# A four-layer network on one core: layer 1's bands from one row at the end of the preparation, a bias table shared with GpSimd, and layer 1's first image in the input weights' place

## The chip, the core and the metric

The kernel runs as one launch on one core of a Trainium2 chip. A core has five engines that run their own instruction lists side by side: TensorE (PE, matrix products into PSUM), VectorE (DVE), ScalarE (ACT), GpSimd (POOL) and SyncE (SP, which here only issues DMAs). Each takes its list strictly in order, so an instruction that waits for a semaphore holds all that stands behind it on its engine. DMAs are issued from SP, ACT and POOL. The metric is the device time of the launch in microseconds (us).

## The reference

The input `x` is 4 x 8 x 512 x 512 in float32. Four layers follow each other, and each adds its result to its own input after a group normalisation (`_gn`, four groups of two channels).

```python
def lif(x):
    def step(v, xt):
        v = v + (xt - v) / TAU
        spk = (v >= V_TH)
        v = v * (1.0 - spk)
        return (v, spk)
    _, s = jax.lax.scan(step, jnp.zeros_like(x[0]), x)
    return s
...
q, k, v = (heads(lif(bn(x @ W.T))) for each of q, k, v)
scores = jnp.einsum('tbhnd,tbhmd->tbhnm', q, k) * scale
bias = bias_table[rel].transpose(2, 0, 1)
scores = scores + bias[None, None]
out = jnp.einsum('tbhnm,tbhmd->tbhnd', scores, v)
out = lif(out)
out = out * gate_scale + gate_shift
out = lif(bn(out @ Wp.T))
...
x = x + layer0(_gn(x))        # the attention above
x = x + conv13x13(_gn(x), w)  # layer 1, one kernel per channel, reflected border
x = x + conv3x3_quantised(_gn(x))
x = x + conv3x3(_gn(x))
```

The first block is shortened: `lif` also has a surrogate for gradients that doesn't change its value, and the line for q, k, v stands for three.

## The kernel before

**Layer 0** works through 32 steps `(b, t)`, b over 8 channels and t over 4 time steps. In a step, four tiles of 128 x 512 of x are transposed on PE and normalised on DVE into `xn` (`transpose`), and multiplied with the input weights `w_v`, `w_k` and `w_q` in this order, four column blocks each (`project_in`, L464: PE multiplies, DVE takes `potential` and the spikes, GpSimd adds a constant to the state). `attend` forms k'v (`ps_kv`), multiplies it with q (`ps_a`, L492), and adds the position bias times v (`ps_b`, L500), for which the bias table is held three times in bfloat16, `toep` 0 to 2: the rounded value, the rounded rest, and the rest of that. `project_out` (L527) multiplies with the output weights `wp` and writes the sum to DRAM as layer 1's input `x1d`, with reflected borders. The loop runs with n from -1: it attends to step n and projects step n + 1. The loads of x (SP, ten buffers) go into the order of the loop.

Ahead of it stands the **preparation**. `load(0)` brings the first x; `bands1` builds layer 1's bands; the three weights are loaded from ACT's queue; `statistics` counts group 0 (`bn_stats`, L393) and `norm_of` makes mean and `grstd` from it: sum, matmul `gps_x` (L178), subtraction, squares, sum, matmul, power on GpSimd (L195). `prepare_in` scales a weight with its batch norm (`diag` L310, `ps_free` L311, multiplication L323, ACT's doubling L324). `prepare_bias` fills `toep` (loads L335, casts on ACT L339, L341 and L343, subtractions on DVE L340 and L342), two heads in flight, since `hankel` and `rest` have two slots each. `prepare_out` scales the output weights and splits them in two (L375 to L381). Where the code says `issue_after`, the order of issue is held behind the named instruction; else a scheduler orders instructions by its own estimate of when they are ready, and the order on each engine is fixed when the kernel is built.

**bands1** makes the matrices by which layer 1's 13 x 13 convolution becomes matrix products: for each of 16 output rows of a window, four products of a constant that slides the taps (`c13`) with the taps of all channels (L673), 64 products in all, copied out of PSUM by ACT and DVE (L682) into a tile in `h_q`'s place, and written to DRAM as `band1d` (L686), since the place is needed again.

**Layer 1** (`Layer1`) is made after layer 0's tiles are given up. It loads `band1d` and an identity `eye` (L706, L709, SP), loads the taps again, sums them (`w_rows`, `ps_sum` L719, `w_sum` L721) and runs 32 images `(b, t)`. For each image SP loads two halves of 917 KB (L732), DVE makes `bt`, the band of channel b times the image's normalisation `r1`, plus the identity (L740), PE multiplies (L750, 64 records), ACT adds `off` on the way out (L757), DVE takes statistics (L759 to L761), and ACT and POOL write to `x2d` (L766). Three image buffers and four PSUM banks rotate. `norm1(3)`, which normalises the last group of layer 0's output, and `weights23`, which prepares layers 2 and 3, stand in the code behind image group 0, but the scheduler is free to put their instructions ahead of it.

**Layers 2 and 3** run interleaved after layer 1 and write the output.

Of the kernel before, what the change touches and what calls it, by code (L numbers as in the profile page):

```python
# [42 lines left out]
P = 128  # L43
T, B, N, D, H = 4, 8, 512, 512, 8
DH = D // H
NC = N // P
# [80 lines left out]
def network(ctx: ExitStack, tc: tile.TileContext, i: dict, out: bass.AP):  # L127
# [81 lines left out]
    band1d = tc.dram_tile([K1_P, B * SHIFTS * M1], F32, name="band1d")  # L209
# [9 lines left out]

    with ExitStack() as s:  # L220
        layer0(s, tc, i, x_in, x1d, ident, block, avg, group_stats, st1, norm1, band1d)
# [15 lines left out]
    with ExitStack() as s:  # L237
        ps_1 = s.enter_context(pool("ps_2", space=PSUM))
        layer1 = Layer1(s, tc, i, x1d, x2d, avg, group_stats, r1, mr1, st2, m2, r2, most, band1d, ps_1, pool)
        layer1.group(0)  # L240
        for g in range(1, G):
            if g == 1:
                norm1(G - 1, ps_1)
                w23 = weights23(tc, i, late, early["y"], ps_1, ident)
            layer1.group(g)
        layer1.next_norm(G - 1)
    with ExitStack() as s:
        layers23(
            s, tc, x2d, out, ident, ind, mask2, avg_same, group_steps, m2, r2, most, w23, early, pool
        )  # L250


def layer0(s, tc, i, x_in, x1d, ident, block, avg, group_stats, st1, norm1, band1d):
# [9 lines left out]
    wT = {n: wpool.tile([P, NC, D], F32, name=f"w_{n}") for n in "vkq"}  # L263
# [16 lines left out]
    def load_weights(n):  # L280
        nc.scalar.dma_start(wT[n], i[f"wT_{n}"].rearrange("(c p) e -> p c e", p=P))
# [44 lines left out]
    def prepare_bias():  # L326
# [6 lines left out]
        for h in range(H):  # L333
# [8 lines left out]
            nc.vector.tensor_sub(r, r, dst[1])  # L342
# [244 lines left out]

    load(0)
    bands1(tc, i, band1d, ps_mm, work, state)
    load_weights("v")  # L590
# [3 lines left out]
    load_weights("k")  # L594
    load_weights("q")
    for k in range(NC):
        transpose(0, k)
    prepare_in("v")
    first = [prepare_in("k")]
    h_of = {n: state.tile([P, NC, N], F32, tag=f"h_{n}", name=f"h_{n}") for n in "vkq"}  # L600
    for n in range(-1, last + 1):
        b, t = steps[max(n, 0)]
        if n >= 0:
            with tc.issue_after(did) if n == 0 else ExitStack():
                so = attend(spikes, t)
            residual = load_x(b, t, "xr")
        if n + 1 <= last:
# [9 lines left out]
            if g + 1 < G:  # L617
                t_next, pair = divmod(j, PAIR)
                statistics(
                    g + 1, t_next, pair, load_x((g + 1) * PAIR + pair, t_next, "xs")  # L620
                )
        for a, name in enumerate("vkq"):
            for c in range(NC):
                if n + 1 <= last:
                    did = project_in(name, c, xns[n + 1], spikes, steps[n + 1][1])
                if (n, name, c) == (-1, "v", 0):
                    first += [did, potentials[0]]
# [14 lines left out]
        if n < 0:  # L642
            with ExitStack() as behind:
# [3 lines left out]
                prepare_out(load_out())  # L647
            for name in "op":
                h_of[name] = state.tile([P, NC, N], F32, tag=f"h_{name}", name=f"h_{name}")


def bands1(tc, i, band1d, psum, work, state):

    nc = tc.nc
    n_w, n_c = K1 + 2 * (PH - 1), i["c13"].shape[1]
    both = work.tile([K1, n_c + B * n_w], F32, tag="q", name="c13")
    c13 = both[:, :n_c]
    nc.scalar.dma_start(c13, i["c13"])
    w1 = both[:, n_c:].rearrange("k (c d) -> k c d", c=B)
    nc.vector.memset(w1, 0.0)  # L660
    taps = w1[:, :, PH - 1 : PH - 1 + K1]
    nc.scalar.dma_start(taps, i["w1"].rearrange("k (c d) -> k c d", c=B))

    band = state.tile([K1_P, B, SHIFTS, M1], F32, tag="h_q", name="band1")
    n_r = 4
    n_s = SHIFTS * PH
    c13 = c13.rearrange("k (f j) -> k f j", f=PH)
    for r0 in range(0, W1_OUT, n_r):
        ps = psum.tile([K1_P, n_r, B, n_s], F32, tag="mm", name="ps_band")
        for r in range(r0, r0 + n_r):  # L670
            at = (W1_OUT - 1 - r) * PH
            for f in range(PH):
                nc.tensor.matmul(  # L673
                    ps[:, r - r0, :, :].rearrange("p c z -> p (c z)"),
                    lhsT=c13[:, f, at : at + K1_P],
                    rhs=w1[:, :, f : f + n_s],
                    start=f == 0,
                    stop=f == PH - 1,
                )
        for z in range(SHIFTS):  # L680
            copy = nc.vector.tensor_copy if z % 2 else nc.scalar.copy
            copy(  # L682
                band[:, :, z, r0 * PH : (r0 + n_r) * PH].rearrange("p c (r o) -> p c r o", o=PH),
                ps[:, :, :, z * PH : (z + 1) * PH].rearrange("p r c o -> p c r o")[:, :, :, ::-1],
            )
    nc.scalar.dma_start(band1d, band.rearrange("p c s m -> p (c s m)"))  # L686


class Layer1:
    def __init__(  # L690
        self, s, tc, i, x1d, x2d, avg, group_stats, r1, mr1, st2, m2, r2, most, band1d, ps_1, pool
# [4 lines left out]
            r2=r2, most=most, ps_1=ps_1,  # L696
        )
        self.ps_c = s.enter_context(pool("ps_c", 4, space=PSUM))
        wpool = s.enter_context(pool("w1"))
# [5 lines left out]
        self.band = wpool.tile([K1_P, B, SHIFTS, M1], F32, name="band1")  # L705
        nc.sync.dma_start(self.band.rearrange("p c s m -> p (c s m)"), band1d)  # L706
        self.eye = wpool.tile([K1_P, SHIFTS, M1], F32, name="eye")
        n_eye = SHIFTS * M1
        nc.sync.dma_start(  # L709
            self.eye.rearrange("p s m -> p (s m)"), i["c128"][:K1_P, i["c128"].shape[1] - n_eye :]  # L710
        )
        taps = wpool.tile([K1, B, K1], F32, name="taps")
# [489 lines left out]
```

## Time and profile before

| | |
|---|---|
| median of 3 runs | 3027.5 us (3026.57 to 3029.91) |
| profiled execution | 3032.56 us, span 3030.8 us, mean PE clock 0.984 |
| PE busy | 2915.8 us (96%) |
| DVE busy | 2212.7 us (73%) |
| ACT busy | 553.9 us (18%) |
| POOL busy | 1039.8 us (34%) |
| first projection (L464) | at 52.2 us |
| layer 0 ends, layer 1's products begin | 2117.1 us, 2131.9 us |
| layer 1's products end | about 2583.9 us |

A busy time is the time in which an engine had an instruction in work. Matmul ends are modelled, so a busy PE is not one at its peak, and an average over the span hides that each stage has a limit of its own. A product in float32 shows as two records. Times of single instructions come from one profiled execution, and its span is compared with itself; the runs give the time.

### The profile page before, as it was taken

What the parts mean: (1) busy time and instruction counts of PE and PEld (TensorE: products, weight loads), DVE (VectorE), ACT (ScalarE), POOL (GpSimd) and SP (SyncE); (2) the same over time, 40 slices, a digit from 0 to 9 for tenths busy, and PEclk for the clock granted to TensorE, in tenths of its full rate; (3) what the DMA queues carried; (4) which work ended last, traced back from release to release, by engine and by line L of the source; (5) the groups of instructions that cost most, each with busy time, mean ns of one, the idle gap of its engine ahead of it and who ended that gap; (6) DMA issues with size and microseconds to landing.
All of it is one profiled execution on the core that took longest, in us unless ns stands there. A gap on an engine that the chain in (4) does not pass through costs nothing. (4 is left out here: it accounts for less than half of the span.)

```text
span 3030.8 us, 38824 instructions
## 1 busy us (share of the span) xinstructions
PE 2915.8 (96%) x13993; PEld 1450.6 (48%) x13993; DVE 2212.7 (73%) x3793; ACT 553.9 (18%) x867; POOL 1039.8 (34%) x1963
## 2 busy tenths in 40 slices
PE   8999999999999999999999999999899999688989
PEld 6555555555555555555555555555333333234433
DVE  5997688788769868867976886786555556886760
ACT  1400010000000001000000000100111111766664
POOL 1242233333224323323422433332211112676651
PEclk9999999999999999999999999999899999889999
DMA  5222222221212222222221111111877878698986
GB/s 185 74 85 64 71 71 64 64 67 61 84 57 71 64 64 71 70 64 64 68 61 55 46 54 50 50 50 44 207 216 199 215 210 239 144 189 216 227 195 172
DMA packets 275702, 327.37 MB, mean 108 GB/s; under 512 B 23600, under 2 KB 171192, under 8 KB 275285
## 3 DMA queue, kind: packets, MB, share of 16 engines
q1 hardware_dynamic: 211930, 235.77, 29.0%
q0 software_dynamic: 23776, 62.35, 7.5%
q10 hardware_dynamic: 39803, 26.77, 3.0%
q8 instruction: 110, 1.80, 0.3%
q14 instruction: 83, 0.68, 0.1%
HBM read 210.60 MB, written 103.17 MB: 104 GB/s over the span
## 5 line engine op out<-in xcount | busy, mean ns | idle before, releaser
L464 PE MATMUL ps_in<-w_v,xn 128*128 128x512 f32 x1024 | 460.7, 599 | 2.5 <-issue 2.2
L464 PE MATMUL ps_in<-w_k,xn 128*128 128x512 f32 x1024 | 450.2, 592 | 1.0 <-DVE v_k L429 0.7
L464 PE MATMUL ps_in<-xn,w_q 128*128 128x512 f32 x1024 | 449.6, 592 | 0.1
L750 PE MATMUL ps_conv<-x,bt 112*64 112x512 f32 x2048 | 445.4, 594 | 0.0
L500 PE MATMUL ps_b<-toep,vtok 128*64 128x512 bf16 x3072 | 371.8, 382 | 0.0
L412 ACT ACTIVATE h_q<-v_q,c_half 128x512 f32<-128x512 f32 x96 | 69.3, 722 | 1543.6 <-DVE v_q L408 1222.3
L549 POOL COPY x1s<-x1s 128x2 f32<-128x2 f32 (+1 forms) x1024 | 226.5, 275 | 295.6 <-DVE x1s L538 295.6
L437 POOL TENSOR_TENSOR h_v<-h_v,c_v 128x512 f32<-128x512 f32 x96 | 123.0, 1281 | 575.3 <-DVE h_v L436 540.8
L527 PE MATMUL ps_out<-wp,so 128*128 128x512 f32 x1024 | 308.8, 444 | 0.0
L1104 PE MATMUL ps_conv<-x,band_t 64*64 64x512 f32 x2040 | 271.7, 609 | 30.2 <-POOL x L1097 14.3
L464 PEld LDWEIGHTS ps_in<-w_k,xn 128*128 128x128 f32 x1024 | 194.1, 190 | 222.4 <-issue 204.7
L464 PEld LDWEIGHTS ps_in<-xn,w_q 128*128 128x128 f32 x1024 | 191.8, 190 | 220.1 <-issue 212.9
L464 PEld LDWEIGHTS ps_in<-w_v,xn 128*128 128x128 f32 x1024 | 190.0, 190 | 216.4 <-issue 211.0
L750 PEld LDWEIGHTS ps_conv<-x,bt 112*64 112x64 f32 x2048 | 150.1, 135 | 286.7 <-issue 286.4
L500 PEld LDWEIGHTS <-vtok 128*64 128x64 bf16 x3072 | 209.5, 110 | 124.0 <-issue 3.6
L527 PEld LDWEIGHTS ps_out<-wp,so 128*128 128x128 f32 x1024 | 192.5, 188 | 94.0 <-issue 58.3
L967 POOL COPY u<-x 128x512 f32<-128x512 f32 (+1 forms) x172 | 200.2, 1197 | 108.0 <-DMA x<-x 71.8
L538 DVE SCALAR_TENSOR_TENSOR x1s<-v_p,xr 128x256 f32<-128x256 f32 x256 | 186.5, 769 | 14.4 <-DMA x<-x1s 3.1
L766 POOL DMA_DIRECT2D x<-xo x128 | 71.4, 564 | 341.1 <-ACT xo L757 326.6
L1104 PEld LDWEIGHTS ps_conv<-x,band_t 64*64 64x64 f32 x2040 | 105.1, 135 | 145.5 <-issue 93.7
L195 POOL TENSOR_TENSOR grstd_x<-grstd_x,neg_half 128x1 f32<-128x1 f32 (+1 forms) x28 | 21.9, 784 | 437.7 <-DVE grstd_x L194 435.6
L757 ACT ACTIVATE xo<-ps_conv,off 128x512 f32<-128x512 f32 x128 | 88.0, 688 | 445.8 <-PE ps_conv L750 387.0
(182 smaller groups left out, 3664.2 us busy)
## 6 DMA issues: line engine op xcount, KB each, us to landing
x<-x SPq DMA_DIRECT2D x64, 917.0 KB
x<-x SPq DMA_DIRECT2D x168, 256.0 KB
x<-x1s POOLq DMA_DIRECT2D x128, 262.0 KB, 2.6
x<-in_x SPq DMA_DIRECT2D x128, 256.0 KB
xr<-in_x SPq DMA_DIRECT2D x128, 256.0 KB
out<-o SPq DMA_DIRECT2D x164, 192.0 KB
xs<-in_x SPq DMA_DIRECT2D x112, 256.0 KB
x<-xo ACTq DMA_DIRECT2D x128, 128.0 KB
```

What stands on the lines that cost most here:

```text
L412: nc.scalar.activation(h, v, AF.Identity, bias=c_col, scale=0.5)
L437: nc.gpsimd.tensor_add(h, h, c_twice[n])
L464: mm = nc.tensor.matmul(ps, lhsT=lhsT, rhs=rhs, start=k == 0, stop=k == NC - 1)
L500: nc.tensor.matmul(pb[two * DH : (two + 1) * DH, :], lhsT=v[:, c, h * DH : (h + 1) * DH], rhs=toep[z][:, h, u : u + N], start=c == 0 and z ...
L527: nc.tensor.matmul(ps, lhsT=so[:, k, c * P : (c + 1) * P], rhs=wpT[z][:, k, :], start=k == 0 and z == 0, stop=k == NC - 1 and z == 1,)
L538: nc.vector.scalar_tensor_tensor(own, v.rearrange("p (g v) -> p g v", g=PH)[:, two, :], 1.0, by_phase[:, two, :], op0=ALU.is_ge, op1=ALU.add,)
L549: nc.gpsimd.tensor_copy(x1[:, f, u : u + n], x1[:, fm, um - n + 1 : um + 1][:, ::-1])
L750: nc.tensor.matmul(ps[q * M1 : (q + 1) * M1, :], lhsT=bt[:, z, :], rhs=xt[:, w0 : w0 + N_PS1, z : z + NV], start=z == 0, stop=z == SHIFTS - 1,
L757: nc.scalar.activation(xo[:, a, :], ps, AF.Identity, bias=off[:, t : t + 1])
L766: engine.dma_start(bass.AP(dst.tensor, dst.offset + (q * n_half * W1_OUT * B + b) * D + f * NV, [[B * D, W1_OUT], [W1_OUT * B * D, n_half] ...
L967: nc.gpsimd.tensor_copy(u[:n_p, j, :].rearrange("p (v g) -> p v g", g=PH), x[:, j, :].rearrange("p (g v) -> p v g", g=PH),)
L1104: mm = nc.tensor.matmul(ps[j][b * HALF : (b + 1) * HALF, :], lhsT=band[half, b, dx, :], rhs=x3[half, s0 + j, dx : dx + D], start=dx == 0, ...
```

## The change

Layer 1's bands are no longer built row by row. `bands1` makes one row by four products into 52 partitions, fills `band1d` with zeros by a DMA from a small zero tile, and writes the row 16 times on top of it, each time four partitions and 128 elements further on, by one DMA whose source is repeated. It also sums the taps (`w_sum`) there, and loads `eye`. It stands as the last part of the preparation, and its scratch is in `h_p`'s place. The element order of the band changes, so `bt` is made by four DVE instructions of 112 x 64 instead of one of 112 x 256.

The second subtraction of the bias table goes from DVE to GpSimd. `w_v` is loaded from SP behind the first x; `w_k` and `w_q` are loaded once `w_v` is prepared, and `k` is prepared behind v's first projection. The statistics of the next group for n = -1 go behind the preparation of the output weights.

The input weights move to a pool that outlives layer 0. In the last step, `w_v`'s place takes the band, and the place of `w_k` and `w_q` takes layer 1's first image; its `bt` is made there too. `norm1(3)` and `weights23` are held behind the first image's last product and last statistic.

```diff
-    band1d = tc.dram_tile([K1_P, B * SHIFTS * M1], F32, name="band1d")
+    band1d = tc.dram_tile([K1_P, W1_OUT * B * SHIFTS * PH], F32, name="band1d")
...
             if g == 1:
-                norm1(G - 1, ps_1)
-                w23 = weights23(tc, i, late, early["y"], ps_1, ident)
+                with ExitStack() as behind:
+                    for op in layer1.started:
+                        behind.enter_context(tc.issue_after(op))
+                    norm1(G - 1, ps_1)
+                    w23 = weights23(tc, i, late, early["y"], ps_1, ident)
...
-    wT = {n: wpool.tile([P, NC, D], F32, name=f"w_{n}") for n in "vkq"}
+    n_x1 = W1_N * X1_U
+    wv = shared.tile([P, NC * D], F32, tag="v", name="w_v")
+    wkq = shared.tile([P, max(2 * NC * D, n_x1)], F32, tag="kq", name="w_kq")
...
-            nc.vector.tensor_sub(r, r, dst[1])
+            nc.gpsimd.tensor_sub(r, r, dst[1])
...
+    def start_layer1():
+        band = shared.tile([K1_P, W1_OUT, B, SHIFTS, PH], F32, tag="v", name="band1")
+        nc.sync.dma_start(band.rearrange("p r c s o -> p (r c s o)"), band1d)
+        x = shared.tile([K1_P, W1_N, X1_U], F32, tag="kq", name="x1_0_0")
+        load_image(nc, x, x1d[0][0])
+        bt = shared.tile([K1_P, SHIFTS, M1], F32, name="bt_0_0")
+        image_bands(nc, bt, band, 0, r1[:, 0, 0:1], eye)
+        return band, eye, x, bt
...
     load(0)
-    bands1(tc, i, band1d, ps_mm, work, state)
-    load_weights("v")
+    load_weights("v", nc.sync)
     statistics(0, 0, 0, xs[0])
     statistics(0, 0, 1, load_x(1, 0, "xs"))
     batch_norms()
-    load_weights("k")
-    load_weights("q")
     for k in range(NC):
         transpose(0, k)
-    prepare_in("v")
-    first = [prepare_in("k")]
+    with tc.issue_after(prepare_in("v")):
+        load_weights("k", nc.scalar)
+        load_weights("q", nc.scalar)
+    first = []
...
             residual = load_x(b, t, "xr")
+            if n == last:
+                head = start_layer1()
...
                 if (n, name, c) == (-1, "v", 0):
-                    first += [did, potentials[0]]
+                    first += [prepare_in("k"), did, potentials[0]]
...
                 prepare_out(load_out())
+                next_group(n)
+                bands1(tc, i, band1d, w_sum, eye, ps_mm, state)
...
+    nc.vector.memset(zeros, 0.0)
+    rest = band1d.rearrange("p (r m) -> p r m", r=W1_OUT)
+    nc.scalar.dma_start(rest, zeros.unsqueeze(1).to_broadcast([K1_P, W1_OUT, P]))
+    ps = psum.tile([n_p, P], F32, tag="mm", name="ps_band")
+    for f in range(PH):
+        nc.tensor.matmul(
+            ps, lhsT=c13[:, f, :], rhs=w1[:, :, f : f + n_s], start=f == 0, stop=f == PH - 1
+        )
+    nc.vector.tensor_copy(
+        band.rearrange("p (m o) -> p m o", o=PH), ps.rearrange("p (m o) -> p m o", o=PH)[:, :, ::-1]
+    )
+    row = W1_OUT * P
+    nc.scalar.dma_start(
+        bass.AP(band1d.tensor, band1d.offset, [[row, n_p], [PH * row + P, W1_OUT], [1, P]]),
+        band.unsqueeze(1).to_broadcast([n_p, W1_OUT, P]),
+    )
+    nc.vector.tensor_reduce(rows, w1, AX.X, ALU.add)
+    nc.vector.memset(zeros[:K1, :], 1.0)
+    ps = psum.tile([P, B], F32, tag="mm", name="ps_sum")
+    nc.tensor.matmul(ps, lhsT=zeros[:K1, :], rhs=rows, start=True, stop=True)
+    nc.vector.tensor_copy(w_sum, ps)
...
-        bt = self.bp.tile([K1_P, SHIFTS, M1], F32, tag="bt", name=f"bt_{b}_{t}")
-        nc.vector.scalar_tensor_tensor(
-            bt, self.band[:, b, :, :], self.r1[:K1_P, g, t : t + 1], self.eye,
-            op0=ALU.mult, op1=ALU.add,
-        )
+        if (b, t) == (0, 0):
+            xt, bt = self.head
+        else:
+            xt = self.xp.tile([K1_P, W1_N, X1_U], F32, tag="x", name=f"x1_{b}_{t}")
+            load_image(nc, xt, self.x1d[t][b])
+            bt = self.bp.tile([K1_P, SHIFTS, M1], F32, tag="bt", name=f"bt_{b}_{t}")
+            image_bands(nc, bt, self.band, b, self.r1[:, g, t : t + 1], self.eye)
```

## The prediction

> **What bounds the kernel now.** I read the busy slices first. TensorE (PE) is at 9 tenths in nearly every slice of layers 0 and 1, so what counts there is where it idles or does work that could go. A table by stretches (columns after the length: PE, weight loads, DVE, ACT, POOL busy, each with a count; granted clock; DMA share; GB/s) finds two such places:
>
> ```profile
> 0.00:10.00 10.00, 2.82 (x13) 2.85 (x14) 3.43 (x12) 0.00 (x0) 4.41 (x8) 1.00 0.80 267
> 10.00:20.00 10.00, 10.00 (x49) 10.00 (x48) 5.61 (x14) 1.55 (x2) 0.00 (x0) 1.00 1.05 391
> ...
> 120.00:130.00 10.00, 6.63 (x30) 3.20 (x30) 9.55 (x18) 6.41 (x11) 0.00 (x0) 0.85 0.26 81
> ...
> 2120.00:2130.00 10.00, 1.18 (x4) 1.00 (x4) 8.50 (x23) 0.00 (x0) 7.71 (x23) 0.52 0.81 184
> 2130.00:2140.00 10.00, 8.71 (x26) 3.44 (x28) 2.08 (x11) 0.00 (x0) 1.04 (x1) 0.63 1.04 208
> ```
>
> The timeline of the start says what the "busy" PE does there (start, length, engine, line, operation):
>
> ```profile
> 7.18 13.96 PE L673 MATMUL ps_band<-c 13*112 13x128 f32 x64 [7.18 <-DVE st L393]
> 15.72 0.17 DVE L175 TENSOR_REDUCE gsum_x<-st 128x1 f32<-128x16 f32 x1
> 21.07 0.59 PE L178 MATMUL gps_x<-gsum_x,avg 128*128 128x1 f32 x2
> 23.40 13.99 PE L673 MATMUL ps_band<-c 13*112 13x128 f32 x64
> 38.18 0.55 POOL L195 TENSOR_TENSOR grstd_x<-grstd_x,neg_half 128x1 f32<-128x1 f32 x1 [30.98 <-DVE grstd_x L194]
> 52.23 2.04 PE L464 MATMUL ps_in<-w_v,xn 128*128 128x512 f32 x2 [2.19 <-issue]
> ```
>
> The reader should see 128 records of layer 1's bands ahead of everything. The statistics of the first tile were summed at 15.7 but their two matmuls stood behind 14.0 us of bands each, so the first projection began at 52.2. The chain that ended last shows the second place, the passage from layer 0 to layer 1 (start, length, what):
>
> ```profile
> 2117.11 3.88 DMA x<-x1s
> ...
> 2126.67 0.60 PE ps_sum L719 x2
> ...
> 2131.30 0.59 PE gps_x L178 x2
> 2131.88 45.07 PE ps_conv L750 x192
> ```
>
> Layer 0's last matmul ends at 2117.1; the convolution begins at 2131.9, behind ps_sum and norm1's gps_x, which are in front of it on PE. From 2122 to 2136 the finer table gives a clock of 0.50.
>
> **What the Trainium skill says.** "TensorE: Matmul & The Clock Gate", What's actually happening: an idle array falls to half clock and wins full clock back by sustained work. The trace agrees: 0.50 above, and x192 took 45.07 us where later x64 take 13.88, so 41.6; 3.4 us were lost. "SBUF — State Buffer", Who interferes with whom: a DVE instruction with two SBUF inputs and a GpSimd one that reads SBUF block each other for a whole instruction. The trace fits: the 128x896 subtraction takes 1.08 us, but 1.56 at times, and GpSimd's 128x512 addition 1.27, or 2.0 while those run. "DMA: Bandwidth & Descriptors", Anatomy of one DMA: about 2 us are fixed, most of it confirmation of the write. A bias-table load took 3.8 us from issue (56.4) to the cast that waited for it (60.2), with data. "GPSIMD Engine Reference", Elementwise: a two-input operation costs about twice DVE's. Here 1.27 against 0.7, so it agrees.
>
> **Part by part: the start.** (1) Bands leave the front: 128 records, 27.9 us of PE, 16 copies. Of w_v, w_k and w_q only w_v now loads at once, on SP behind x; so before the statistics are complete 3.4 MB must come (x, w_v, xs at 1.05 each, constants 0.2). At the table's 267 GB/s for 10 us and 391 after, that is 11.8 us, against 15 now. The last bn_stats ends at 12.5. The chain (reduce, matmul, copy, three small DVE steps, reduce, matmul, add, power) is some 4 us by its rows; four w_v multiplications of 0.62 stand between its steps: 18.7. Then xn at 0.80: first projection at about 20, 32 us earlier. (2) Some is given back. k's preparation, formerly ahead of the projections, now stands behind v's first: eight diag of 0.24 and four multiplications (2.5 us) on DVE, while PE's second group waits for their steps; w_k is issued only after v's preparation (19), so it lands near 26. DVE also gets four bn_stats (2.5 us) of xs that it used to do at 16 to 21, when idle. Stepping through both queues gives 22 us for v's phase instead of 16.4: k starts at 42 instead of 68.6, 26 earlier. (3) Bias table: eight L342 subtractions (1.08) leave DVE, 8.6 us, and become GpSimd's, at 896/512 x 1.27 = 2.2 us free, 3.3 if blocked as above. But ACT takes its casts in order, toep_2 of a head ahead of toep_1 of the next, so a pair of heads costs six casts (5.6), two GpSimd subtractions and one of DVE: 11 us. In the trace pairs start at 69.0, 81.4, 90.7, 99.9, about as far apart. So the last cast stays some 23 us earlier: 86.5, not 109.4. (4) The preparation's tail, where the trace shows PE waiting for ACT behind the output weights:
>
> ```profile
> 124.47 0.59 ACT L510 ACTIVATE v_o<-ps_a 128x512 f32<-128x512 f32 x1
> 125.11 0.41 PE L492 MATMUL ps_a<-q,kvb 128*64 128x512 f16 x2 [2.62 <-ACT v_o L510]
> ```
>
> gets the new bands: 10 small matmul records, DVE about 1.1 us (two memsets, reduce, copy, memset, copy), and four loads and writes on ACT. ACT's write of the band waits for the 896 KB of zeros to land, with the wp casts behind it; DVE's memset of ones waits for the same, with the weights' second pass and the next tile's xn behind; ps_sum on PE waits for that memset, with v's next projection behind. The zeros go out in 512 B pieces. Layer 1 moves such pieces at 242 GB/s in its densest stretch: 3.8 us, and 2 fixed, 7 with the input loads beside it. PE waits 4 to 5 us there, but DVE's wp work ends hardly earlier, so 1 to 4 us stick. Upper bound: a 128 KB write from POOL lands in 5.9 us in the issue table; seven of these in a row would be 41. I take 7. So PE's third head pair starts at 106, not 126.5: **20 us** gained, bounds 8 and 28 (32 less the 4 that must stick).
>
> Hidden: statistics moved by half a step in layer 0 (PE is busy 298.9 of 300 us from 1200 to 1500); the eye load, 112 KB on ACT.
>
> **The passage.** The band (SP, waits for w_v's last reader) is read back behind the xr loads. Its bt stands on DVE directly behind an x1s; w_v's last matmul starts near 2063, 896 KB take about 5 us, DVE gets there after 6: 0 to 1 us. The image goes where w_k and w_q were, released at 2096: two loads of 917 KB, 9 us at 200 GB/s, ready by 2107. The convolution then follows ps_out as soon as DVE has read the last two ps_out (1.39 us from 2116.5): 2118.0 instead of 2131.9. That is 13.9 us, exactly one image of PE time, and 3.4 us of clock. SP's next image now waits for tiles read last at 2109 (toep), not for the eye load (25.6 us of SP waiting now); it lands well before 2132. norm1 and weights23 go behind image 0 on DVE, which is busy 54 us of 100 in layer 1; their two gps_x cost PE 0.8 us there. bt becomes four 112x64 instead of one of 0.48 us; at up to 0.3 each that is 0.7 more of a 13.9 us image: hidden. **16.5 us**, bounds 11 and 17.5.
>
> Sum: 20 + 16.5 = 36.5 from the span of 3030.8, so 2994; this execution was 3032.6 by the clock of the runs, 0.17% over their median of 3027.5. Taken off the median: **2991**. Layers 2 and 3 move along unchanged.
>
> **Rivals.** (a) The tail is worse: zeros of 15 to 20 us, or GpSimd's subtractions above 3.3 us, eat 8 to 13 of the start: 2999 to 3005. For: DVE is full from 60 to 100 already (10.00, 9.56, 10.00, 9.88). Against: GpSimd is idle there half the time. (b) The start comes almost whole: 28 to 30, 2981. For: PE's order puts other work into the waits. Against: the in-order casts. (c) The passage fails: image 1 is late, as its second half was issued 8 us after the first in this trace, behind another queue's load: 20 alone, 3007. Against: its queue slots are old ones. (d) Slower: the zeros hold ACT, DVE and PE at once. Only above 7 + 36.5 = 43.5 us does that turn the sign, and 50 us for 0.2% (6 us); even 41 leaves 3025. (e) That the change doesn't do what it says: excluded for the order of PE, where L673's records are gone from the front.
>
> **How the numbers follow.** Forecast 2984 to 2999: 0.66. (a) 0.14, (b) 0.11, (c) 0.03, no change 0.03, (d) 0.03. Range 2981 to 3004 leaves out about a fifth: the far ends of (a) and (b), (c), no change and (d). No change means within 0.2%, about what a measurement of this kernel can tell.
>
> **What would show it.** First ps_in<-w_v near 20; k's near 42; last toep cast near 86; ps_a's wait for ACT near 104; ps_conv within 2 us of the last ps_out and no clock of 0.5 after it. A ps_sum wait above 10 us, DVE idle on a bands write, or a hole after image 0 would make it wrong.

## The result, and the profile after

The changed kernel takes 3004.6 us (median of 4 runs, 3004.4 to 3006.8); the kernel before took 3028.7 in the 4 runs beside it. The ratio is 0.9919, with a 95% interval of 0.9902 to 0.9936. It is faster by 24 us; the forecast was 36.5 us and 2991 (2981 to 3004). The marks in one row of the tables below come from one profiled execution. Two executions of one kernel differ by some 2 us in the start (170.3 and 172.4 below). Over all kernels, whatever their edit, the rest of layer 0 (second step to last ps_out) varies by 6.5 us, and layers 2 and 3 from 439 to 449 us. So the start and the passage are read from the trace, and the whole from the ratios.

Four marks in the trace carry what follows: ACT's first `v_o` of the third pair of heads (end of the preparation), the first `v_o <- ps_a` on DVE of the second time step, the start of layer 0's last `ps_out`, and from there to the start of the last `ps_conv` record of layer 1 (passage and layer 1).

| us | first v_o | second step | last ps_out | to last ps_conv |
|---|---|---|---|---|
| before | 124.5 | 183.2 | 2116.7 | 466.5 |
| after | 111.2 | 170.3 | 2105.5 | 451.5 |
| forecast, by its sum | 104 | 163 | 2096.7 | 450.0 |

The lines behind the first two rows (the first v_o of before stands in the prediction; in the view by tile the figures are count, shortest/median/longest ns, first and last start), first before, then after:

```profile
183.18 0.69 DVE L512 SCALAR_TENSOR_TENSOR v_o<-ps_a,h_o 128x512 f32<-128x512 f32 x1
L527 PE MATMUL ps_out<-wp,so x1024: 388/394/799, 133.9 to 2116.7; 128*128 128x512 f32 x171
...
170.32 0.68 DVE L533 SCALAR_TENSOR_TENSOR v_o<-ps_a,h_o 128x512 f32<-128x512 f32 x1
L548 PE MATMUL ps_out<-wp,so x1024: 388/395/801, 118.9 to 2105.5; 128*128 128x512 f32 x171
L797 PE MATMUL ps_conv<-x,bt x2048: 589/591/644, 2106.0 to 2557.0; 112*64 112x512 f32 x187
```

The passage brought 15.0 of the 16.5 us expected. The start brought 13.3, 12.9 and 11.2 where 20 were expected. The table of stretches of the kernel after (columns as ahead of the prediction) shows both:

```profile
0.00:10.00 10.00, 3.35 (x11) 2.10 (x12) 4.17 (x17) 1.28 (x1) 4.41 (x8) 1.00 0.79 268
10.00:20.00 10.00, 5.27 (x19) 4.01 (x18) 7.50 (x23) 0.03 (x1) 0.55 (x1) 1.00 0.64 226
90.00:100.00 10.00, 6.75 (x45) 4.56 (x45) 8.00 (x23) 2.12 (x3) 0.96 (x1) 0.94 0.63 177
100.00:110.00 10.00, 8.40 (x18) 4.34 (x19) 7.76 (x15) 2.71 (x5) 0.55 (x1) 0.72 0.55 152
...
2110.00:2120.00 10.00, 9.96 (x48) 3.04 (x44) 4.88 (x15) 0.16 (x1) 6.58 (x20) 1.00 0.78 184
```

From 90 to 110 PE, DVE and ACT are all part idle, and the clock falls to 0.72. That fits a wait for something outside them. At the passage nothing is left of the clock of 0.50. PE's timeline says where the start's gain stood at each point:

```profile
21.58 1.91 PE L485 MATMUL ps_in<-w_v,xn 128*128 128x512 f32 x2
...
43.91 1.45 PE L485 MATMUL ps_in<-w_kq,xn 128*128 128x512 f32 x3
...
101.60 0.56 PE L738 MATMUL ps_sum<-bands 13*128 13x8 f32 x2 [3.75 <-DVE gsum_x L175]
...
112.71 0.82 PE L521 MATMUL ps_b<-toep,vtok 128*64 128x512 bf16 x5
...
169.40 0.41 PE L513 MATMUL ps_a<-q,kvb 128*64 128x512 f16 x2 [3.34 <-DVE kvb L506]
...
2106.00 13.95 PE L797 MATMUL ps_conv<-x,bt 112*64 112x512 f32 x64
2120.59 1.94 PE L797 MATMUL ps_conv<-x,bt 112*64 112x512 f32 x8 [0.63 <-ACT xo L804]
```

v starts 30.7 us earlier than before, k 24.7, as forecast within 2 us. The third pair of heads starts at 112.7, 13.8 earlier and not 20; before it was at 126.5:

```profile
126.48 3.97 PE L500 MATMUL ps_b<-toep,vtok 128*64 128x512 bf16 x20
```

So the loss lies between, and a little more follows at 169. ACT's own timeline (ACTq is its issuing of DMAs) shows what it waited for:

```profile
94.48 0.69 ACTq L719 DMA_DIRECT2D band1d<-bands  x1
...
101.05 0.37 ACTq L730 DMA_DIRECT2D band1d<-bands  x1
101.46 1.14 ACT L400 CAST wp<-wp_k 128x512 fp32r<-128x512 f32 x2 [5.66 <-DVE gsum_x L175]
...
111.24 0.59 ACT L531 ACTIVATE v_o<-ps_a 128x512 f32<-128x512 f32 x1
```

L719 writes the zeros to DRAM, L730 the row of bands into them. L730 is issued 6.57 us after L719, as it must wait until the zeros have landed, and ACT's casts of the output weights stand behind it. (The releaser printed, gsum_x, is not it: in the second execution of this kernel the view names the DMA of band1d at this place, with 5.60 us.) ACT's first `v_o` of the third pair stands at the end of that row of casts, at 111.24.

### The profile page after: what moved, and what is told of

It is laid out like the page before. It is cut to its first block, busy times and chain, and to the rows that moved or that the text cites. A ratio compares the mean times of both kernels' runs of the same rounds, so it can differ in the third digit from the quotient of the medians.

```text
span 3002.9 us, 38667 instructions
## 1 busy us (share of the span) xinstructions
PE 2889.0 (96%) x13873; PEld 1426.6 (48%) x13873; DVE 2225.3 (74%) x3875; ACT 551.0 (18%) x859; POOL 1054.3 (35%) x1971
## 5 line engine op out<-in xcount | busy, mean ns | idle before, releaser
L485 PE MATMUL ps_in<-xn,w_kq 128*128 128x512 f32 x1024 | 453.0, 595 | 4.8 <-DVE v_q L441 3.7
L485 PE MATMUL ps_in<-w_kq,xn 128*128 128x512 f32 x1024 | 450.1, 593 | 1.6 <-DVE v_k L450 1.6
L485 PEld LDWEIGHTS ps_in<-w_kq,xn 128*128 128x128 f32 x1024 | 194.3, 190 | 223.1 <-issue 205.3
L485 PEld LDWEIGHTS ps_in<-xn,w_kq 128*128 128x128 f32 x1024 | 192.1, 191 | 227.4 <-issue 211.8
L1153 PE MATMUL ps_conv<-x,band_t 64*64 64x512 f32 x2040 | 276.1, 612 | 24.4 <-ACT o L1162 13.8
L1016 POOL COPY u<-x 128x512 f32<-128x512 f32 (+1 forms) x172 | 198.2, 1185 | 104.5 <-DMA x<-x 56.7
L1153 PEld LDWEIGHTS ps_conv<-x,band_t 64*64 64x64 f32 x2040 | 112.3, 136 | 135.9 <-issue 94.2
L1051 PE MATMUL ps_conv<-xq,band 64*64 64x512 bf16 x1020 | 138.8, 399 | 32.1 <-DVE xq L1031 32.0
```

Source lines behind the costliest of these rows:

```text
L485: mm = nc.tensor.matmul(ps, lhsT=lhsT, rhs=rhs, start=k == 0, stop=k == NC - 1)
L1016: nc.gpsimd.tensor_copy(u[:n_p, j, :].rearrange("p (v g) -> p v g", g=PH), x[:, j, :].rearrange("p (g v) -> p v g", g=PH),)
L1051: mm = nc.tensor.matmul(ps[half, :], lhsT=w["band2"][half, 0, dx, :], rhs=xq[half, j, dx + 1 : dx + 1 + D], start=dx == 0, stop=dx == 2,)
L1153: mm = nc.tensor.matmul(ps[j][b * HALF : (b + 1) * HALF, :], lhsT=band[half, b, dx, :], rhs=x3[half, s0 + j, dx : dx + D], start=dx == 0, ...
```

## The experiments

All edits are to the changed kernel unless another base is named. Theory: the missing 8 to 9 us of the start are lost (T1) to GpSimd's subtractions, (T2) to the zeros and the bands at the end of the preparation, (T3) to the moved statistics. The marks of all runs, and the ratio to the kernel before:

| us | first v_o | second step | last ps_out | to last ps_conv | ratio, 95% interval |
|---|---|---|---|---|---|
| after | 111.2 | 170.3 | 2105.5 | 451.5 | 0.9919, 0.9902 to 0.9936 |
| after, again | 113.2 | 172.4 | 2106.4 | 452.0 | 0.9917, 0.9901 to 0.9932 |
| subtraction on DVE | 106.8 | 168.8 | 2104.4 | 452.1 | 0.9917, 0.9902 to 0.9932 |
| zeros early | 107.0 | 163.9 | 2096.3 | 451.6 | 0.9886, 0.9868 to 0.9904 |
| zeros early, again | 105.9 | 162.8 | 2095.8 | 450.9 | 0.9904, 0.9887 to 0.9920 |
| no bands | 104.9 | 162.9 | 2096.4 | 451.5 | 0.9881, 0.9864 to 0.9897 |
| statistics early | 114.7 | 175.3 | 2112.7 | 451.8 | 0.9940, 0.9924 to 0.9956 |
| zeros early, k early | 110.2 | 167.1 | 2101.7 | 451.4 | 0.9901, 0.9884 to 0.9918 |
| zeros early, DVE | 104.5 | 163.9 | 2099.8 | 452.2 | 0.9885, 0.9869 to 0.9902 |
| zeros early, in pairs | 108.9 | 166.6 | 2100.1 | 451.8 | 0.9884, 0.9860 to 0.9907 |
| ones of their own | 112.1 | 171.7 | 2105.2 | 451.6 | 0.9924, 0.9909 to 0.9938 |
| row from GpSimd | 108.5 | 171.0 | 2102.4 | 451.5 | 0.9915, 0.9900 to 0.9929 |
| kvb first | 110.7 | 167.0 | 2101.5 | 451.4 | 0.9908, 0.9893 to 0.9923 |
| row from GpSimd, kvb first | 105.0 | 164.0 | 2094.9 | 451.3 | 0.9879, 0.9864 to 0.9894 |
| image late | 112.5 | 172.2 | 2108.9 | 460.6 | 0.9947, 0.9929 to 0.9964 |
| whole passage back | 114.0 | 173.0 | 2109.9 | 460.4 | 0.9954, 0.9938 to 0.9969 |

**Subtraction on DVE.**

```diff
-            nc.gpsimd.tensor_sub(r, r, dst[1])
+            nc.vector.tensor_sub(r, r, dst[1])
```

> The changed kernel with the second subtraction of the bias table back on VectorE, all else as it is (3004.6 us there). Theory T1, that the missing 9 us of the start go to GpSimd's eight subtractions (VectorE stretched from 0.42 to about 2 us beside them, and ScalarE's in-order casts waiting 2 to 4 us for each of them): the last bias cast ends 3 to 6 us before 91.9, and the time is 2999 to 3002. Rival, the forecast's own sum (a pair of heads 11 us with GpSimd, more without): the table ends later, 94 to 97, and the time is 3007 to 3010.

The last cast of the table began at 84.0 instead of 91.0: GpSimd makes the table 7 us later. But TensorE's wait at ps_sum grew from 3.75 to 7.5 us, and the ratio is the same, 0.9917. Each theory had half of it: the table was earlier, the time was not. That GpSimd's cost was only hidden behind the zeros was the next guess; the run with both edits, below, doesn't bear it out.

**Zeros early.** `zeros` is the still empty tile of `eye`; the sum of the taps takes the existing `ones`.

```diff
                         statistics(0, 1, 1, load_x(1, 1, "xs"))
+                        zeros = eye.rearrange("p s m -> p (s m)")[:, :P]
+                        nc.vector.memset(zeros, 0.0)
+                        nc.sync.dma_start(band1d..., zeros.unsqueeze(1).to_broadcast(...))
...
-    nc.scalar.dma_start(rest, zeros.unsqueeze(1).to_broadcast([K1_P, W1_OUT, P]))
...
-    nc.vector.memset(zeros[:K1, :], 1.0)
```

> The changed kernel with the zeros of layer 1's bands written to DRAM early, from the still empty tile of eye, on SyncE's queue behind the first potential, and the existing tile of ones in place of the rewritten zeros; the row of bands itself stays at the end of the preparation. Theory T2, that TensorE's wait of 3.75 us at ps_sum (the ones are written only when the fill has landed) and ScalarE's 5.7 us before the casts of the output weights are on the path: that wait is gone and the time is 3000 to 3002. Rival: the path through the end of the preparation is the bias table and VectorE, and the wait lies beside it: 3003.5 to 3005.

ACT's timeline with the zeros early:

```profile
98.97 0.62 ACT L400 CAST wp<-wp_k 128x512 fp32r<-128x512 f32 x1 [1.19 <-DVE wp_k L396]
...
100.25 0.36 ACTq L732 DMA_DIRECT2D band1d<-bands  x1
...
106.95 0.59 ACT L531 ACTIVATE v_o<-ps_a 128x512 f32<-128x512 f32 x1
```

The casts start before the row is written, not behind it. Layer 0 ends at 2096.3, 20.4 us before the kernel before: the forecast's 20. That is more than T2 expected, so the zeros cost more than the one wait. All eight runs of this kernel (2991.0 to 3001.90, both of its rows in the table) lie below all nine of the changed kernel (3001.92 to 3009.5), the nearest two by hardly anything.

**Bands left out.** As zeros early, and the row of bands isn't made: layer 1 works with empty filters (band zero, `w_sum` one), with the same instructions.

```diff
-    ps = psum.tile([n_p, P], F32, tag="mm", name="ps_band")
...
-    nc.vector.tensor_copy(w_sum, ps)
+    nc.vector.memset(w_sum, 1.0)
```

> The changed kernel with the zeros written early and the row of bands left out altogether (band stays zero, w_sum is set to one, so layer 1 is computed with empty filters; the instructions of the layers are the same). This is the most that moving the bands away from the end of the preparation can bring. Theory T2: 4 to 6 us less than the changed kernel, 2998.5 to 3000.5. Rival, that the loss lies before 92 (GpSimd) or after 112: 3003 to 3005.

No gain over the zeros early at the end of layer 0 (2096.4 and 2096.3). The row itself costs next to nothing; its zeros do.

**Statistics early.**

```diff
-            if n >= 0:
-                next_group(n)
+            next_group(n)
...
-                next_group(n)
                 bands1(tc, i, band1d, w_sum, eye, ps_mm, state)
```

> The changed kernel with the second group's first statistics (four loads of xs and their VectorE work) back at their old place, ahead of v's first projection. Theory T3, that moving them behind the preparation pushes the next loads of xs into the first time step, where VectorE waits 1.9 us for them and TensorE 3.3 us at 169 for kvb: that wait is gone, v's projections start up to 1 us later, and the time is 3002 to 3003.5. Rival, that the moved work was in the way of the first projections: those start 3 us later (near 25) and the time is 3006 to 3009.

The rival came nearer. v's first projection wasn't later (20.5), but the marks are 2 to 7 us later and TensorE still waited 3.1 us for kvb. By the marks it was a gain that these statistics moved (the intervals of the ratios overlap), and their move is not what makes kvb late.

**k early**, with the zeros early.

```diff
-    with tc.issue_after(prepare_in("v")):
-        load_weights("k", nc.scalar)
-        load_weights("q", nc.scalar)
-    first = []
+    prepare_in("v")
+    first = [prepare_in("k")]
```

and the two loads straight behind `batch_norms()`.

> The kernel with the zeros written early (2993.7 us in its own runs), with k's weights loaded on ScalarE's queue straight behind the statistics and prepared ahead of v's projections, as in the kernel before. Theory, that k's late preparation (TensorE waits 2.6 us for VectorE's scaled weights of k, and k starts at 46.4 where the forecast said 42) costs the start: k starts 2 to 3 us earlier, and the time is 1 to 3 us less. Rival, that VectorE and ScalarE with the bias table set the pace from 50 on, and the wait for k only moves: v's first projection is later (25 to 28), the table ends at 91 as before, and the time is within 1 us or up to 3 us more.

v starts at 32.2, k at 47.6 (46.4), the second step 3 to 4 us later. The rival, and a little more than it said (2998.0 against 2993.7 and 2997.2; the ratios don't tell them apart): by the marks, loading k behind v was right, and TensorE's 2.6 us for k's weights are the small price.

**Image late.** Image (0, 0) is taken from layer 1's pools like the others; band and eye stay ahead.

```diff
-        x = shared.tile([K1_P, W1_N, X1_U], F32, tag="kq", name="x1_0_0")
-        load_image(nc, x, x1d[0][0])
...
-        if (b, t) == (0, 0):
-            xt, bt = self.head
-        else:
+        if True:
```

> The changed kernel with layer 1's first image and its bands taken from layer 1's own pools again, as all later images are (band and eye stay loaded ahead). Theory, the forecast's passage: the image can be loaded only when layer 0's pools have been given back, so that TensorE stands 8 to 14 us after its last product of layer 0, and restarts with a lower clock; last product of layer 0 at 2105.9 as in the changed kernel, first of layer 1 near 2118; time 12 to 17 us more. Rival, that band and eye were the long part of it: the image's load alone costs 4 to 8 us.

9.1 us more from the last ps_out to the end of layer 1; 8 by the times. PE's timeline shows where:

```profile
2101.58 7.76 PE L548 MATMUL ps_out<-wp,so 128*128 128x512 f32 x32
2110.51 1.93 PE L791 MATMUL ps_conv<-x,bt 112*64 112x512 f32 x4 [1.18 <-DVE bt L755]
2116.66 1.98 PE L791 MATMUL ps_conv<-x,bt 112*64 112x512 f32 x4 [4.22 <-DMA x<-x]
```

Four records find their half of the image, the next wait 4.2 us for the other, and from 2118 to 2122 the clock is 0.50. That is less than the theory's 12 to 17, and at the upper end of the rival's 4 to 8: the image is the larger part, but not all.

**Zeros early, subtraction on DVE**: both edits.

> The kernel with the zeros written early, and the second subtraction of the bias table back on VectorE as well. Theory T1 and T2 together: the table ended 7 us earlier without GpSimd, which was hidden behind the zeros (TensorE's wait at ps_sum grew from 3.7 to 7.5 us); with neither, the last cast ends near 85, TensorE's third pair of heads comes 4 to 7 us earlier than the 108.1 with the zeros early, and layer 0 ends near 2091: 2987 to 2990 us. Rival, that VectorE, which then does eight subtractions of 1.05 us more, is the limit at the end of the preparation too: layer 0 ends within 2 us of 2096, and the time is that of the zeros early, 2991.5 to 2995.

The rival. The ACT cast groups of the view by tile (count, shortest/median/longest ns, first and last start), first of the zeros early, then with the subtraction on DVE too:

```profile
L364 ACT CAST toep<-rest x8: 922/938/939, 55.5 to 91.2; 128x896 bf16<-128x896 f32 x8
```

```profile
L364 ACT CAST toep<-rest x8: 922/938/940, 53.1 to 82.7; 128x896 bf16<-128x896 f32 x8
```

The table ends 8.5 us earlier, the first v_o comes 1.4 to 2.5 us earlier, and the second step begins at the same 163.9. With the eight subtractions DVE is busy for 19.96 of the 20 us from 60 to 80.

**Casts in pairs**, with the zeros early: `prepare_bias` issues both first casts of a pair of heads, then both second, then both third.

```diff
+            for src, r, dst, h in pair:
+                nc.scalar.copy(dst[1], r)
+                nc.gpsimd.tensor_sub(r, r, dst[1])
+            for src, r, dst, h in pair:
+                nc.scalar.copy(dst[2], r)
```

> The kernel with the zeros written early, GpSimd still doing the second subtraction, but the bias table issued for two heads at once: both first casts, both second casts, both third casts, so that ScalarE has a cast of the other head to do while GpSimd subtracts. Theory, that ScalarE's wait in order is what GpSimd costs (17.1 us idle behind the second cast in the kernel with the zeros early): the table ends 4 to 7 us earlier, near 86, and layer 0 ends 3 to 6 us earlier. Rival, that VectorE's stretched instructions beside GpSimd are the cost: the table ends within 2 us of 92.1 and the time is within 1.5 us of the zeros early.

The last cast began at 91.6, against 91.2. The rival: ACT's order isn't what GpSimd costs. DVE's stretched instructions are what is left; they were not tried by themselves.

**The changed kernel again, the ones alone, the whole passage back**, on one chip.

> The changed kernel itself once more, beside the next two on one chip, so that they have a neighbour: 3002 to 3007 us, and the second time step's first potential of layer 0 (170.3 in its first profile) at 169 to 173.

> The changed kernel with one edit: the sum of the taps takes the tile of ones that exists already, instead of overwriting the zeros when their fill has landed. The fill stays where it is, and so does ScalarE's wait for it before the write of the row. Theory, that the part of the fill that counts is VectorE's and TensorE's wait in order (3.75 us at ps_sum, and the statistics and the next loads of xs behind it, 3.3 us at 169): most of the 10 us of the early fill is had, 2994 to 2998. Rival, that ScalarE's queue is what counts (idle 5.7 us until 101.5, then the casts of the output weights): 3000 to 3004.

```diff
-    nc.vector.memset(zeros[:K1, :], 1.0)
-    nc.tensor.matmul(ps, lhsT=zeros[:K1, :], rhs=rows, start=True, stop=True)
+    nc.tensor.matmul(ps, lhsT=ones[:K1, :], rhs=rows, start=True, stop=True)
```

The changed kernel's second execution came as expected (3006.3 us, second step 172.4). For the ones alone it is the rival's direction (3008.7 us, above its range): the wait at ps_sum is gone, and nothing is gained. ACT's timeline has stayed as it was:

```profile
96.05 0.70 ACTq L719 DMA_DIRECT2D band1d<-bands  x1
...
102.70 0.37 ACTq L730 DMA_DIRECT2D band1d<-bands  x1
103.11 1.14 ACT L400 CAST wp<-wp_k 128x512 fp32r<-128x512 f32 x2 [5.74 <-DMA band1d<-bands]
```

Here the view names the DMA itself.

```diff
+        self.band = wpool.tile([K1_P, W1_OUT, B, SHIFTS, PH], F32, name="band1")
+        nc.sync.dma_start(self.band.rearrange("p r c s o -> p (r c s o)"), band1d)
+        self.eye = wpool.tile([K1_P, SHIFTS, M1], F32, name="eye")
...
-        if (b, t) == (0, 0):
-            xt, bt = self.head
```

> The changed kernel with the whole passage back as it was: band, eye and first image are loaded by SyncE from layer 1's own pools after layer 0's have been given back; only the sums of the taps stay in the preparation. Taking the image back alone cost 9 us (459.0 instead of 451.0 us of layer 1, and 1.1 us ahead of it). Theory, that band and eye ahead of the image in the queue make the rest of the 15: last product of layer 0 to the end of layer 1 is 466 to 468 us instead of 451.5, and the time 3017 to 3021. Rival, that the rest was the taps and their sum (TensorE waited 9.6 us for them before), which stay done here: 460 to 462 us, 3011 to 3015.

Band, eye and image come from layer 1's pools again, and are loaded there. 460.4 us, and 3017.2 in the time: no more in the passage than the image alone. The rival: band and eye cost nothing beside the image, so the other 6 us of the 15 must belong to what stayed changed, the sum of the taps in the preparation and `norm1` and `weights23` behind image 0.

**The row written from GpSimd**, with the ones of their own:

```diff
-    nc.scalar.dma_start(
+    nc.gpsimd.dma_start(
         bass.AP(band1d.tensor, band1d.offset, [[row, n_p], [PH * row + P, W1_OUT], [1, P]]),
```

> The changed kernel with the tile of ones that exists already, and with the write of the row of bands issued by GpSimd instead of ScalarE; the fill stays at the end of the preparation on ScalarE's queue, and the write still waits for it, but on GpSimd, which has little to do there. With the ones alone changed the time was that of the changed kernel. Theory, that ScalarE's wait is what counts: its casts of the output weights begin near 98 instead of 101.5 to 103.1, the third pair of heads gets its first v_o from ScalarE at 106 to 108 (111.2 to 113.2 in the changed kernel), and the second time step's first potential comes at 164 to 167; 2994 to 3000 us. Rival, that VectorE's work on the output weights ends no earlier (the forecast's reason to let only 1 to 4 us stick): v_o at 110 to 113, and 3002 to 3006.

The casts of the output weights began no earlier than in the changed kernel (101.5 and 103.0), though the write no longer stands on ACT's queue:

```profile
102.58 0.62 ACT L400 CAST wp<-wp_k 128x512 fp32r<-128x512 f32 x1 [5.60 <-DVE wp_k L396]
```

Now they wait for DVE, whose first pass over the output weights (L396) began at 101.4, behind statistics that waited 0.86 us for their load. So ACT's long idle time is not what the write costs: in the changed kernel, where that first pass began at 99.2, the casts' input was late as well. The first v_o came at 108.5, between the two theories; what is earlier is DVE's second pass (L401, at 103.6 instead of 106.7), which here stands ahead of work that waits for PE. The second step came at 171.0, no earlier than in the changed kernel. What was won at 108 was lost again in TensorE's wait for kvb:

```profile
170.03 0.41 PE L513 MATMUL ps_a<-q,kvb 128*64 128x512 f16 x2 [3.28 <-DVE kvb L506]
```

That wait is in all kernels so far with the zeros at the end (2.9 to 3.3 us) and in none with the zeros early. In the changed kernel DVE's timeline at that place reads:

```profile
161.72 0.69 DVE L414 BATCH_NORM_STATS2 st<-xs 128x6 f32<-128x512 f32 x1 [1.29 <-DMA xs<-in_x]
...
165.03 0.69 DVE L414 BATCH_NORM_STATS2 st<-xs 128x6 f32<-128x512 f32 x1 [0.31 <-DMA xs<-in_x]
...
168.66 0.68 DVE L506 TENSOR_TENSOR kvb<-ps_kv,c 128x512 f16<-128x512 f32 x1
```

Statistics for later time steps stand ahead of kvb, and wait for their loads. In the kernel before none stands in the 9 us ahead of kvb, and they follow it:

```profile
171.37 0.69 DVE L393 BATCH_NORM_STATS2 st<-x 128x6 f32<-128x512 f32 x1 [0.74 <-DMA x<-in_x]
...
181.92 0.69 DVE L485 TENSOR_TENSOR kvb<-ps_kv,c 128x512 f16<-128x512 f32 x1
182.52 0.68 DVE L393 BATCH_NORM_STATS2 st<-x 128x6 f32<-128x512 f32 x1
```

**kvb first**, alone and with the row from GpSimd: the statistics of later steps are issued behind kvb.

```diff
-                statistics(0, n + 2, 0, xs[n + 2])
-                statistics(0, n + 2, 1, load_x(1, n + 2, "xs"))
+                more = load_x(1, n + 2, "xs")
+                with tc.issue_after(kvbs[-1]):
+                    statistics(0, n + 2, 0, xs[n + 2])
+                    statistics(0, n + 2, 1, more)
```

> The changed kernel with one edit: the statistics of the third and fourth time step are issued behind kvb of the attention of that step, as they stand in the kernel before. Theory, that the order of VectorE's instructions is a loss of its own: TensorE's wait of 3.3 us for kvb at 169 is gone, the second time step's first potential comes at 166 to 169 instead of 170.3 to 172.4, and the time is 3000.5 to 3003. Rival, that the wait only moves to the next load of x or xs: 3004 to 3007.

> The kernel with the row of bands written by GpSimd and the ones of their own, and the same order of the statistics behind kvb; the fill stays at the end of the preparation. Theory, that ScalarE's wait (4 us) and the order (3 us) are the two halves of what the early fill gave: first v_o of the third pair at 107 to 109, second time step's first potential at 163.5 to 166.5, as with the early fill (163.9), and 2994 to 2998 us. Rival, that the fill's own traffic beside the loads of x is the rest: 168 to 171, and 2999 to 3003.

> The kernel with the zeros written early once more, beside the two above on one chip: second time step's first potential at 163 to 166, last product of layer 0 at 2095 to 2100, and 2991 to 2997 us.

Alone, the order brings the second step from 170.3 and 172.4 to 167.0, as the theory said (3000.0 us). It works in the preparation too, where a kvb of the first step stands: DVE's first pass over the output weights begins at 96.1 instead of 99.2, and ACT's casts at 97.3, no longer behind the write. Yet the first v_o is hardly earlier (110.7, against 111.2 and 113.2). What is left there is TensorE's wait at ps_sum for the rewritten zeros, DVE's for gps_x, which stands behind it on TensorE, and ACT's for DVE:

```profile
102.02 0.56 PE L740 MATMUL ps_sum<-bands 13*128 13x8 f32 x2 [3.71 <-DVE bands L738]
108.15 0.16 DVE L183 COPY gmean_x<-gps_x 128x1 f32<-128x1 f32 x1 [3.86 <-PE gps_x L178]
110.21 0.62 ACT L400 CAST wp<-wp_k 128x512 fp32r<-128x512 f32 x1 [6.67 <-DVE wp_k L396]
```

With the ones of their own and the row from GpSimd as well this chain of waits is gone or under 0.7 us, the first v_o is at 105.0, and the time is below what was expected (2990.3). The second step comes at 164.0, as with the zeros early (163.9, 162.8), and layer 0 ends at 2094.9. TensorE's timeline has no wait at kvb:

```profile
161.29 2.13 PE L521 MATMUL ps_b<-toep,vtok 128*64 128x512 bf16 x17
163.49 0.41 PE L513 MATMUL ps_a<-q,kvb 128*64 128x512 f16 x2
```

So the zeros cost two things: the waits until they have landed, on ACT, DVE and PE, and an order of DVE's instructions that goes with them. Each alone brings little or part, both together all. How the waits divide is not shown: the ones of their own together with the order, without the row on GpSimd, were not run, and the lines above speak for PE's wait at least as much as for ACT's. This version (median 2990.3 us, ratio 0.9879) and the one with the zeros early (2993.7 and 2997.2) take less than the changed kernel and the one before; their intervals overlap, so which of the two is better is open.

## Why the prediction was wrong

**What bounds the kernel: right.** The two places named, the front and the passage, are where the gain came from, and the rival with its sign turned was far off.

**Step (1), first projection near 20: right** (21.6). **Step (2), k at 42: right within 2 us** (43.9). The phase between took 22.3 us where 22 were forecast.

**Step (3), the table: the mechanism was wrong, and it didn't matter.** The last cast was put at 86.5 by ACT's order in a pair of heads; it ended at 91.9. Casts in pairs changed nothing, so ACT's order doesn't set it. Without GpSimd the table ended at 83.6 to 85. The forecast costed GpSimd's subtraction at 2.2 us, 3.3 if blocked; seven of the eight take 1.88 to 2.06, one 2.73. What it left out is what DVE pays beside it; that this lengthens the table is the reading that is left, not one that was tried by itself. It counted DVE instructions with two SBUF inputs; the timeline shows casts with one SBUF input held as well:

```profile
54.68 1.88 POOL L363 TENSOR_TENSOR rest<-rest,toep 128x896 f32<-128x896 f32 x1
55.20 1.65 DVE L490 TENSOR_SCALAR k<-v_k 128x512 bf16<-128x512 f32 x1
...
62.77 2.06 POOL L363 TENSOR_TENSOR rest<-rest,toep 128x896 f32<-128x896 f32 x1
63.02 2.37 DVE L457 SCALAR_TENSOR_TENSOR h_k<-v_k 128x512 f32<-128x512 f32 x1
```

L490 takes 0.41 us alone and L457 0.68; both end 0.3 to 0.6 us after GpSimd does. The Trainium skill's "SBUF — State Buffer", Who interferes with whom, says both: two-input instructions contend, and copies, casts and tensor_scalar can too, in their two-port modes, the other engine being fully blocked. The trace agrees. Yet the time did not depend on it: 0.9917 and 0.9919 with the zeros late, 0.9885 and 0.9886 with them early. On balance this part of the change brought nothing.

**Step (4), the preparation's tail: the step that failed.** The zeros' time was right (7 forecast, 6.6 measured; the fixed 2 us in its sum come from a section on DMAs that GpSimd issues, the fill went out from ACT, and no run separates a fixed part), and so were the three engines held by them. What failed is "DVE's wp work ends hardly earlier, so 1 to 4 us stick". DVE's second pass over the output weights ended at 112.1 and 114.1 in the two executions of the changed kernel, and at 108.3 and 107.2 with the zeros early; the first v_o came 4 to 7 us earlier with it. In all 9.2 us stuck at the end of layer 0 (20.4 us gained with the zeros early, 11.2 so), 10.6 by the second executions. The forecast had named the waits of the three engines one by one, and then let nearly all of them count for nothing. In the changed kernel DVE's second pass stands behind a wait for gps_x, which stands behind ps_sum on PE:

```profile
104.42 0.16 DVE L194 TENSOR_SCALAR grstd_x<-gps_x 128x1 f32<-128x1 f32 x1 [2.03 <-PE gps_x L178]
...
106.69 1.29 DVE L401 TENSOR_TENSOR wp_k<-wp_k,wp 128x512 f32<-128x512 f32 x2
```

That is one strand of several: with the ones of their own this wait is 0.78 us, and the second pass still begins only at 107.6. A part was not in the sum at all. With the zeros at the end DVE's order is another one: its first pass over the output weights begins at 99.2 and 101.2 (97.8 and 96.7 with the zeros early), and in the second time step statistics of later steps stand ahead of kvb, where PE stood 3.3 us. Putting these statistics behind kvb alone was worth 3 to 5 us at the second step, and 6 to 8 together with the waits. ("Hidden: statistics moved by half a step in layer 0" is about other statistics: with those moved back PE still stood 3.1 us at kvb.) Why the scheduler's order changes with the place of the zeros was not tried.

With both undone the start gains 19.2 us at the second step, near the forecast's 20. That is in part luck: the forecast had the table 23 us earlier and took 1 to 4 off for the tail, and the table came only 17 us earlier (last cast ended at 91.9, not 109.4).

**The passage: right in size, its reason only in part.** PE goes from ps_out to ps_conv with 0.1 us between them and no fall of the clock. After the first five images the gain of the passage alone is 16.9 us: the chain of the kernel after has run 320 records by 2176.67,

```profile
2120.59 27.69 PE ps_conv L797 x128
2148.59 13.88 PE ps_conv L797 x64
2162.79 13.88 PE ps_conv L797 x64
2176.67 1.04 PE ps_band L891 x32
```

and that of before had run them by 2206.81, with 2.08 us of ps_band among them: 28.06 less, of which 11.2 come from the start. The other 1.9 are lost in later images, about 0.5 in each eight, and were not located. What the forecast gave to the image (released buffers, an exact image of PE time) is only 9 of the 15. By elimination the rest is the taps' sum, `norm1` and `weights23`, which no longer stand ahead; they were not tried apart.

**The sum.** 20 + 16.5 was forecast, 11.2 + 15.0 came by the first profile, 10.3 + 14.5 by the second. Rival (a), "the tail is worse", had the right time (2999 to 3005) and the wrong reason: the zeros didn't take 15 to 20 us, nor GpSimd over 3.3.

## What to carry to other kernels

When a write must wait for another write, look at what stands behind the wait on every engine that it touches: here three engines were held, and freeing one or two of them did little. The idle time in front of an instruction is not what its wait costs: ACT was idle for 5.7 us ahead of its casts, and with the write off its queue they began no earlier, since their input was late too. An instruction moved out of the way can be placed by the scheduler ahead of something urgent later on; compare the order of each engine at the next stage, not only at the place of the edit. Undo suspected costs in pairs as well as singly: the ones and the row brought nothing at the second step, the order 3 to 5 us, all of them 6 to 8.

## What the runs showed of the hardware

GpSimd's subtraction of two 128 x 896 float32 operands takes 1.88 to 2.06 us in seven cases of eight and 2.73 in one; from the 4497 ns for 2048 elements in the Trainium skill's "GPSIMD Engine Reference", Elementwise, one gets 1.97 as an estimate, so the trace agrees but for the one. A DVE cast of 0.41 us beside it took 1.65 and 2.10. Filling 896 KB of DRAM in pieces of 512 B from one tile took 6.6 us from issue to the release of the write that waited for it (94.48 to 101.05, and 96.05 to 102.70), some 136 KB in a microsecond.
